# A scan layer's gate: projected before the scan and kept in DRAM, or projected behind the scan

## The chip, the cores and the metric

The kernel runs on one core of one Trainium2 chip. The metric is the device time of one launch in microseconds; of several executions the median is taken.

## What is computed

Four layers run one after the other on x of shape (8, 64, 64, 64). The change lies in the first, a selective-scan block. Cut to what matters, for each of 8 images with L = 4096 positions, 64 channels, an inner width of 128 and 16 states:

```python
xz = einsum('bhwc,dc->bhwd', ln(x), in_proj_w) + in_proj_b
xi, z = split(xz, 2, axis=-1)              # z: the gate
xc = silu(dwconv3(xi))
...                                        # four directions k of a scan over L:
h = h * exp(dt_t * A) + dt_t * B_t * u_t   # 128 channels x 16 states
y = sum over k of (C_t . h) + D * u
y = ln(y) * silu(z)                        # normalised over the 128 channels
xh = x + einsum('bhwd,cd->bhwc', y, outproj_w) + outproj_b
```

The layers that follow (a gate with attention, a modifier that is trained for some steps, another attention) take xh and are not touched.

## The kernel before

The scan layer (`scan_layer`, L242) handles the images one by one. An image's scan has 16 steps `s` (the loop at L928): four directions k, each with four chunks of 1024 positions. A step has 16 turns `n`, one for each state (the loop at L958). A turn holds, on its engines:

- ScalarE: `decay` (L733), the exponential for two turns ahead; `save_state` (L769).
- PE and ScalarE: `spread` for the next turn, which fills the PSUM tile z: for most states by matmuls (L751), for the states in `BY_POOL` (0, 3, 6, 8) by a copy of ScalarE (L748) from a product that GpSimd made (L741).
- VectorE: `unit`, a product z * dus in PSUM (L778, not for `BY_POOL`) and the scan (L782) into one of three h buffers.
- GpSimd: the product of h with the broadcast C row (L787); once a step two products for the next step's inputs (L659, L678).
- PE: `sum_up`, which adds that product of three turns before into y's PSUM tile (L848).
- SP: `load`, the broadcast loads of the B and C rows (L729), 512 KB each.

All other work is cut into items, pairs `(make, use)`, that a queue (`Background`, L166) hands out. In each turn `bg.before` calls one item's `make` (mostly a matmul into one of two PSUM banks, `bank`, L331); after the turn's scan `bg.after` first issues what was put off by `bg.later`, and then calls the `use` of the item of the turn before. In turns 6, 7 and 8 no item with a `make` is begun. Convolution parts stand in groups of their own, which alternate with the queue. The order of instructions is thus written out by hand; a tile scheduler adds only the semaphores.

The items that matter here:

- `before(b)` (L489) prepares an image while the image ahead of it is scanned: it loads x into the tile xn (one buffer), normalises it there (`norm_x`, L369), projects it for the convolution (`project_in`, L505), and for the gate: `gate` (L520) has a matmul from xn with the second half of `win` (L524), a Silu of ScalarE from PSUM into the SBUF tile z (L529), and a DMA that puts z into the DRAM tile zd (L530). The eight gates of an image stand in the queue behind its projections; for image 0 they are put in at step 4.
- `after(b)` (L566) finishes an image while the next one is scanned: from step 0 of the next image, turn 4, on. Its items come from `norm_y` (L426): variances of eight blocks of 512 positions (L438, put into the row tile vrow by ScalarE, L344, and into DRAM, L345), the chain over DRAM that makes the inverse root, then for each block `apply` (VectorE y * rps, L460; ScalarE Identity with the norm's scale and bias, L461), `multiply` (GpSimd z * y, L580), and `project_out` (two matmuls, L586 and L587, Identity L593, store L594). `load` (L571) fetches the block of x for the residual and the block of z (L575).
- The last image's blocks are finished two at a time in its own last three steps and behind the last scan; there a turn hands out two items.

An Exp, a Silu, a Ln and a Sqrt of ScalarE need different tables. Where one follows another, an ACT_TABLE_LOAD stands ahead of it.

Of the kernel before, what the change touches and what calls it, by code (L numbers as in the profile page):

```python
# [241 lines left out]
def scan_layer(cm, x_in, w, xh):  # L242

    tc, nc = cm.tc, cm.nc
    with ExitStack() as ctx:
# [177 lines left out]
                    out.append(none)  # L423
            return out

        def norm_y(y, blocks, load, multiply, project_out):  # L426

            put, chain, sm = inverse_root(len(blocks))
            j0, nb, sq = blocks[0], len(blocks), {}

            def square(j):
                sq[j] = work.tile([128, BK], F32, name="sq", tag="sq")
                nc.scalar.activation(sq[j], y[:, bass.ts(j, BK)], AF.Square)

            def variance(j):
                def make():
                    ps = bank("vps1")
                    nc.tensor.matmul(  # L438
                        ps[:1], lno_avg[:, NBK - 1 : NBK], sq.pop(j), start=True, stop=True
                    )  # L440
                    return ps

                def use(ps):
                    put(ps, 1, j - j0)
                    if j + 2 in blocks:
                        square(j + 2)

                return make, use

            def apply(j):  # L450
                def make():
                    ps = bank("rps")

                    row = cm.ident[:nb, j - j0 : j - j0 + 1].to_broadcast([nb, DI])
                    nc.tensor.matmul(ps, row, sm["r"], start=True, stop=True)
                    return ps

                def use(ps):
                    v = y[:, bass.ts(j, BK)]
                    nc.vector.tensor_tensor(v, v, ps, ALU.mult)  # L460
                    nc.scalar.activation(v, v, AF.Identity, bias=on_b, scale=on_g)  # L461
                    if j - 1 in blocks:
                        multiply(j - 1)

                return make, use

            out = [(None, lambda _: [square(j) for j in blocks[:2]]), none]
            for j in blocks:
                out.append(variance(j))
                if j in blocks[1:6:2] or nb == 2:  # L470
                    at = j if nb == 2 else j0 + (j - j0) // 2
                    out.append((None, lambda _, at=at: load(at)))
            out += chain
            out += [apply(j) for j in blocks[:2]]
            end = (None, lambda _: multiply(blocks[-1]))
            if nb == 2:
                out += [end, none]
            for j in blocks:
                if j + 2 in blocks:
                    out.append(apply(j + 2))  # L480
                    if j + 2 == blocks[-1]:
                        out.append(end)
                out += [project_out(j), none]
            return out


# [1 line left out]

        def before(b):  # L489

            xn = io.tile([2 * C, NBK // 2, BK], F32, name="xn", tag="xn", bufs=1)

            def block(j):
                e = j % 2
                return slice(e * C, (e + 1) * C), xn[e * C : (e + 1) * C, j // 2, :]
            u = io.tile([DI, L], F32, name="u", tag="u")
            zd = dr.tile([DI, L], F32, name="zd", tag="zd")
            rows = BK // S

            xs = x_in[b].rearrange("c h w -> c (h w)")  # L500
# [4 lines left out]
            def project_in(j):  # L505
                def make():
                    ps = bank("xps")
                    half, x = block(j)
                    nc.tensor.matmul(ps, win[half, 0, :], x, start=True, stop=True)
                    return ps  # L510

                def use(ps):
                    nc.scalar.activation(
                        pad[:, 1 + j * rows : 1 + (j + 1) * rows, 1 : S + 1],
                        ps.rearrange("p (r c) -> p r c", c=S), AF.Identity, bias=inb[:, 0:1],
                    )

                return make, use

            def gate(j):  # L520
                def make():
                    ps = bank("zps")
                    half, x = block(j)
                    nc.tensor.matmul(ps, win[half, 1, :], x, start=True, stop=True)  # L524
                    return ps

                def use(ps):
                    z = work.tile([DI, BK], F32, name="z", tag="z", bufs=3)
                    nc.scalar.activation(z, ps, AF.Silu, bias=inb[:, 1:2])  # L529
                    bg.later(lambda: nc.sync.dma_start(zd[:, bass.ts(j, BK)], z))  # L530

                return make, use

# [27 lines left out]
            items = [[(None, load(j)) for j in range(NBK)]]  # L561
            for pairs in FIRST if b == 0 else (range(NBK // 2),):
                items.append(norm_x(b, xn, pairs, project_in))
            return u, zd, items, [gate(j) for j in range(NBK)], [convolve(j) for j in range(NBK)]

        def after(b, y, zd, blocks=range(NBK)):  # L566

            xf = x_in[b].rearrange("c h w -> c (h w)")
            gated = {}
# [1 line left out]
            def load(j):  # L571
                xr = work.tile([C, BK], F32, name="xr", tag="xr", bufs=3)
                nc.sync.dma_start(xr, xf[:, bass.ts(j, BK)])
                z = work.tile([DI, BK], F32, name="z", tag="z", bufs=3)
                nc.sync.dma_start(z, zd[:, bass.ts(j, BK)])  # L575
                gated[j] = (xr, z)

            def multiply(j):
                z = gated[j][1]
                nc.gpsimd.tensor_tensor(z, z, y[:, bass.ts(j, BK)], ALU.mult)  # L580

            def project_out(j):
                def make():
                    po = bank("ops")
                    xr, z = gated[j]
                    nc.tensor.matmul(po[:C], cm.ident[:C, :C], xr, start=True, stop=False)  # L586
                    nc.tensor.matmul(po[:C], wout, z, start=False, stop=True)  # L587
                    return po

                def use(po):  # L590
# [6 lines left out]

                return make, use

            return norm_y(y, blocks, load, multiply, project_out)  # L600

        def ordered(t, k, c):

# [290 lines left out]
        later = {}  # L894

        def start(b):
            u, zd, items, gates, convs = before(b)
            images[b] = {"u": u, "zd": zd}
            bg.add(items[0] + items[1])
            if b == 0:  # L900
                bg.add(convs[0] + convs[1])
                for s in range(1, NCH):
                    later[s] = sum(items[s + 1 : s + 2], []) + convs[2 * s] + convs[2 * s + 1]
                later[NCH] = gates
            else:
                bg.done[b] = 0
                bg.add([(None, lambda _: bg.groups.extend(deque(conv) for conv in convs))])
                bg.add(gates)


        with tc.manual_schedule():
# [15 lines left out]
            for b in range(NB):  # L927
                for s in range(4 * NCH):  # L928
# [29 lines left out]
                    for n in range(N):  # L958
# [29 lines left out]

                        if s == 0 and n == LAG + 2 and b > 0:
                            last = images.pop(b - 1)  # L990
                            bg.add(after(b - 1, last["row"], last["zd"]))
                            bg.add([(None, lambda _, b=b - 1: bg.flushed.add(b))])
                        if late and n == LAG + 2:
                            c = 4 * NCH - s
                            bg.add(after(b, images[b]["row"], images[b]["zd"], range(2 * c, 2 * c + 2)))
                        if s == (1 if b else NCH) and n == 0 and b + 1 < NB:
                            bg.add(later.pop(NCH, []))
                            start(b + 1)
                    if nxt:
                        if not nxt["first"]:  # L1000
# [4 lines left out]
                sum_up()  # L1005
            empty()
            last = images[NB - 1]
            bg.add(after(NB - 1, last["row"], last["zd"], range(2)))
            bg.drain()


# [1146 lines left out]
```

## Time and profile before

| what | value |
|---|---|
| median of 3 runs | 12329.48 us (12318.48 to 12333.17) |
| profiled execution, its own time | 12328.75 us |
| span of the profiled execution | 12326.7 us, mean granted PE clock 0.952 |
| scan layer within the span | first scan at 94.4 us, last scan begins at 7016.3 us |
| image 2, first scan to next image's first | 856.3 us |
| DMA in all | 1562.16 MB, 38.5% of 16 engines' span |

The profile is one execution as the hardware profiler recorded it. The page's groups give for each line of the kernel the engine, the operation, its operands with their shapes, the count, and then behind the first bar the busy time in all and the mean time of one in ns, and behind the second bar how long the engine had stood idle just before these instructions and who ended that. A table of windows gives the busy time of each engine in a stretch of the span. A timeline lists an engine's instructions in order (start, duration, and in brackets the idle time ahead of it with its releaser; neighbours of one kind are merged).

### The profile page before, as it was taken

The page shows a single profiled execution, that of the slowest core. Times are in us where ns is not written, and L with a number is a line of the kernel's source. Part 1 is how long each engine was busy: PE and PEld are TensorE (multiplying, and loading weights), DVE is VectorE, ACT ScalarE, POOL GpSimd, SP SyncE. Part 2 cuts the span into 40 slices and gives each one's busy share as a digit, 9 for nine tenths or more (in the row PEclk, how much of TensorE's full clock was granted, in tenths as well). Part 3 has the DMA queues.
Part 4 walks back from the last instruction along what each step waited for, and adds up shares of the span by engine and source line. Part 5 has one row for each costly group of instructions (what it writes and reads, how often), then busy time and mean ns, then how long its engine had stood idle before and what let it go on. Part 6 is the DMA issues. An engine that isn't in the chain of part 4 may idle for free. (4 is left out here: it accounts for less than half of the span.)

```text
span 12326.7 us, 120038 instructions
## 1 busy us (share of the span) xinstructions
PE 11203.1 (91%) x38827; PEld 4075.9 (33%) x38827; DVE 10359.2 (84%) x7334; ACT 7820.8 (63%) x10409; POOL 7399.3 (60%) x3510
## 2 busy tenths in 40 slices
PE   7899999999999999999998899999987779999999
PEld 2233332332332332333322233232335463333333
DVE  5999999999999999999999776868677686676767
ACT  4776776776766766767766554646547574555554
POOL 5999999999999999999999700000006480000000
PEclk8999999999999999999999899999998789999999
DMA  3666666666666666666666400000011100000000
GB/s 115 207 213 218 209 209 217 219 203 216 218 210 213 211 210 217 213 215 213 199 213 211 164 24 26 5 25 7 17 41 41 41 21 24 19 4 19 5 11 6
DMA packets 541331, 1562.16 MB, mean 127 GB/s; under 512 B 127360, under 2 KB 144400, under 8 KB 538128
## 3 DMA queue, kind: packets, MB, share of 16 engines
q1 hardware_dynamic: 540688, 1554.36, 38.5%
q8 instruction: 309, 5.06, 0.2%
q14 instruction: 334, 2.74, 0.1%
HBM read 1456.41 MB, written 88.87 MB: 125 GB/s over the span
## 5 line engine op out<-in xcount | busy, mean ns | idle before, releaser
L787 POOL TENSOR_TENSOR ct<-ct,h 128x1024 f32<-128x1024 f32 x2048 | 4794.6, 2364 | 248.2 <-DVE h L782 113.3
L782 DVE TENSOR_TENSOR_SCAN h<-a,state,z 128x1024 f32<-128x1024 f32 x1536 | 3573.1, 2342 | 118.2 <-ACT z L748 67.1
L1159 DVE TENSOR_TENSOR sum<-sum,ex 128x1024 f32<-128x1024 f32 x1920 | 2347.5, 1223 | 618.1 <-ACT ex L1152 484.4
L1152 ACT ACTIVATE ex<-sc 128x1024 f32<-128x1024 f32 x2048 | 1968.1, 1024 | 1359.6 <-PE sc L1147 1359.6
L848 PE MATMUL yps<-ct,ident 128*128 128x512 f32 x5632 | 2809.0, 630 | 2.5 <-POOL ct L787 2.4
L733 ACT ACTIVATE a<-dt,amat 128x1024 f32<-128x1024 f32 x2048 | 2345.4, 1147 | 725.9 <-DVE h L782 712.5
L778 DVE TENSOR_TENSOR z<-z,e 128x1024 f32<-128x1024 f32 x1536 | 1863.3, 1213 | 221.1 <-PE z L751 143.2
L1166 PE MATMUL av<-ex,v 128*64 128x512 f32 x8192 | 1950.0, 604 | 0.0
L1147 PE MATMUL sc<-q,k 16*128 16x512 f32 (+1 forms) x8192 | 1562.2, 623 | 4.2 <-ACT q L1140 3.1
L848 PEld LDWEIGHTS yps<-ct,ident 128*128 128x128 f32 x5632 | 1006.4, 194 | 1384.2 <-issue 1220.6
L751 PE MATMUL z<-bs,pick 48*128 48x512 bf16 x3072 | 948.0, 389 | 536.5 <-DVE h L782 485.5
L848 PE MATMUL yps<-ct,lno_cen 128*128 128x512 f32 x2560 | 1276.3, 630 | 0.0
L782 DVE TENSOR_TENSOR_SCAN h<-a,z 128x1024 f32<-128x1024 f32 x512 | 1162.7, 2282 | 81.4 <-ACT z L748 57.2
L741 POOL TENSOR_TENSOR bt<-bt,e 128x1024 f32<-128x1024 f32 x512 | 1210.1, 2364 | 5.3 <-DMA bt<-bc 5.3
L1473 POOL TENSOR_TENSOR gt<-gt,pad 128x1024 f32<-128x1024 f32 x16 | 34.9, 2179 | 1570.2 <-ACT gt L1472 1570.2
L1166 PEld LDWEIGHTS av<-ex,v 128*64 128x64 f32 x8192 | 512.2, 136 | 1332.8 <-issue 1278.9
L1147 PEld LDWEIGHTS sc<-q,k 16*128 16x128 f32 (+1 forms) x8192 | 528.4, 184 | 1016.2 <-issue 977.3
L748 ACT COPY z<-bt 128x1024 f32<-128x1024 f32 x512 | 519.8, 1015 | 537.5 <-POOL bt L741 334.8
L751 PEld LDWEIGHTS <-pick 48*128 48x128 bf16 x3072 | 177.6, 95 | 1754.9 <-DVE h L782 1003.0
L848 PEld LDWEIGHTS yps<-ct,lno_cen 128*128 128x128 f32 x2560 | 458.1, 193 | 618.3 <-issue 564.2
L544 PE MATMUL vps<-pad,convd 128*128 128x512 f32 x1152 | 550.9, 602 | 12.9 <-ACT e L648 12.9
L1846 DVE RECIPROCAL r<-e 128x512 f32<-128x512 f32 x128 | 420.7, 3323 | 0.0
(416 smaller groups left out, 10449.5 us busy)
## 6 DMA issues: line engine op xcount, KB each, us to landing
ct<-bc SPq DMA_DIRECT2D x2048, 512.0 KB
bt<-bc SPq DMA_DIRECT2D x512, 512.0 KB
x<-x SPq DMA_DIRECT2D x12, 2048.0 KB
bc<-e SPq DMA_DIRECT2D x128, 128.0 KB
zd<-z SPq DMA_DIRECT2D x64, 256.0 KB
z<-zd SPq DMA_DIRECT2D x64, 256.0 KB
x<-x SPq DMA_DIRECT2D x32, 512.0 KB
part<-x SPq DMA_DIRECT2D x128, 128.0 KB
```

What stands on the lines that cost most here:

```text
L544: nc.tensor.matmul(held[0].rearrange("p (r c) -> p r c", c=S), convd[:, t, :], pad[:, j * rows + dy : (j + 1) * rows + dy, dx : dx + S], s ...
L733: ctl["exp", n] = nc.scalar.activation(ctl["a", n], ctl["dt"], AF.Exp, scale=amat[:, ctl["k"], n : n + 1])
L741: nc.gpsimd.tensor_tensor(bt, bt, ctl["dus"], ALU.mult)
L751: nc.tensor.matmul(z[:, bass.ts(i, BK)], pick[:, n : n + 1].to_broadcast([3 * N, DI]), ctl["bs"][:, bass.ts(i, BK)], start=True, stop=True,)
L778: first = nc.vector.tensor_tensor(z, z, ctl["dus"], ALU.mult)
L782: nc.vector.tensor_tensor_scan(h[:, flip], a[:, flip], z[:, flip], 0.0 if state is None else state[:, n : n + 1], ALU.mult, ALU.add,)
L787: freed[at] = nc.gpsimd.tensor_tensor(ct, ct, h, ALU.mult)
L848: nc.tensor.matmul(ctl["ps"][:, bass.ts(i, BK)], ctl["mat"], ct[:, bass.ts(i, BK)], start=False, stop=(n == N - 1 and not ctl["turns"]),)
L1147: nc.tensor.matmul(sc[:, e, :], k[r : r + d, bass.ts(j, 128)], qs[i][r : r + d, :], start=True, stop=True,)
L1152: nc.scalar.activation(ex, sc, AF.Exp)
L1159: nc.vector.tensor_tensor(sums[i], sums[i], ex, ALU.add)
L1166: nc.tensor.matmul(avs[i][r, :], v[:, j, r], ex[:, e, :], start=(j == 0), stop=(j == TQ - 1))
```

## The change

- The gate is no longer made in `before` and no longer put into DRAM: zd, its 64 stores and 64 loads are gone, and the SBUF tile z with them.
- xn gets two buffers, so that an image's normalised input is still there when its scan has ended.
- `after` has a new `gate(j)`: its `make` has the matmul from xn with `win` into a PSUM bank, and puts off a Silu in place in that bank to the end of the turn; its `use`, one turn later, is a product on VectorE of the bank and y's block, written into y.
- GpSimd's `multiply` is gone; `project_out` reads y instead of z.
- In `norm_y` the gates stand one in a row of three: apply, gate, project. The separate items for `load` are gone; the first three blocks of x are fetched in the `use` of the first three variances.

The core of the diff (the rest are the signatures and the call sites that hand on `block` in place of `zd`):

```diff
@@ norm_y
                     if j + 2 in blocks:
                         square(j + 2)
+                    if j - j0 < 3:
+                        load(j)
...
                     nc.scalar.activation(v, v, AF.Identity, bias=on_b, scale=on_g)
-                    if j - 1 in blocks:
-                        multiply(j - 1)
...
             for j in blocks:
                 out.append(variance(j))
-                if j in blocks[1:6:2] or nb == 2:
-                    at = j if nb == 2 else j0 + (j - j0) // 2
-                    out.append((None, lambda _, at=at: load(at)))
             out += chain
-            out += [apply(j) for j in blocks[:2]]
-            end = (None, lambda _: multiply(blocks[-1]))
-            if nb == 2:
-                out += [end, none]
+            out += [apply(j) for j in blocks[:2]] + [gate(j0)]
             for j in blocks:
                 if j + 2 in blocks:
                     out.append(apply(j + 2))
-                    if j + 2 == blocks[-1]:
-                        out.append(end)
-                out += [project_out(j), none]
+                out += [gate(j + 1) if j + 1 in blocks else none, project_out(j)]
@@ before
-            xn = io.tile([2 * C, NBK // 2, BK], F32, name="xn", tag="xn", bufs=1)
+            xn = io.tile([2 * C, NBK // 2, BK], F32, name="xn", tag="xn")
...
-            zd = dr.tile([DI, L], F32, name="zd", tag="zd")
...
-            def gate(j):
-                def make():
-                    ps = bank("zps")
-                    half, x = block(j)
-                    nc.tensor.matmul(ps, win[half, 1, :], x, start=True, stop=True)
-                    return ps
-
-                def use(ps):
-                    z = work.tile([DI, BK], F32, name="z", tag="z", bufs=3)
-                    nc.scalar.activation(z, ps, AF.Silu, bias=inb[:, 1:2])
-                    bg.later(lambda: nc.sync.dma_start(zd[:, bass.ts(j, BK)], z))
@@ after
-                z = work.tile([DI, BK], F32, name="z", tag="z", bufs=3)
-                nc.sync.dma_start(z, zd[:, bass.ts(j, BK)])
-                gated[j] = (xr, z)
-
-            def multiply(j):
-                z = gated[j][1]
-                nc.gpsimd.tensor_tensor(z, z, y[:, bass.ts(j, BK)], ALU.mult)
+                gated[j] = xr
+
+            def gate(j):
+                def make():
+                    ps = bank("zps")
+                    half, x = block(j)
+                    nc.tensor.matmul(ps, win[half, 1, :], x, start=True, stop=True)
+                    bg.later(lambda: nc.scalar.activation(ps, ps, AF.Silu, bias=inb[:, 1:2]))
+                    return ps
+
+                def use(ps):
+                    v = y[:, bass.ts(j, BK)]
+                    nc.vector.tensor_tensor(v, ps, v, ALU.mult)
...
-                    xr, z = gated[j]
-                    nc.tensor.matmul(po[:C], cm.ident[:C, :C], xr, start=True, stop=False)
-                    nc.tensor.matmul(po[:C], wout, z, start=False, stop=True)
+                    v = y[:, bass.ts(j, BK)]
+                    nc.tensor.matmul(po[:C], cm.ident[:C, :C], gated[j], start=True, stop=False)
+                    nc.tensor.matmul(po[:C], wout, v, start=False, stop=True)
```

In the changed kernel the Silu is at L558, VectorE's gate product at L563, the product y * rps still at L462 and the scan at L767.

## The prediction, made before the changed kernel had run

> **What bounds the kernel now.** I read the page first (busy shares and largest groups), then a table of engine busy time by image, then the idle times in VectorE's own timeline, each with its releaser, image by image, and last what ScalarE was doing at those moments. Everything that the change touches runs in the scan layer, the first 7050 us. I count images 0 to 7, in each 16 steps of 1024 positions, in each step 16 turns n (one scan, L782, is one turn).
>
> The page: the costliest group on each engine.
> ```profile
> PE 11203.1 (91%) x38827; PEld 4075.9 (33%) x38827; DVE 10359.2 (84%) x7334; ACT 7820.8 (63%) x10409; POOL 7399.3 (60%) x3510
> ...
> L787 POOL TENSOR_TENSOR ct<-ct,h 128x1024 f32<-128x1024 f32 x2048 | 4794.6, 2364 | 248.2 <-DVE h L782 113.3
> L782 DVE TENSOR_TENSOR_SCAN h<-a,state,z 128x1024 f32<-128x1024 f32 x1536 | 3573.1, 2342 | 118.2 <-ACT z L748 67.1
> ...
> L778 DVE TENSOR_TENSOR z<-z,e 128x1024 f32<-128x1024 f32 x1536 | 1863.3, 1213 | 221.1 <-PE z L751 143.2
> ```
> Busy time in one image (image 2, from its first scan to the next image's first).
> ```profile
> core 0: us, PE busy (x) PEld busy (x) DVE busy (x) ACT busy (x) POOL busy (x), PEclk, DMA share, GB/s
> ...
> 1868.60:2724.90 856.30, 799.37 (x1824) 271.89 (x1824) 818.62 (x463) 615.34 (x881) 835.78 (x377) 0.97 0.65 213
> ```
> GpSimd is busy 835.8 of 856.3 us and VectorE 818.6: two engines nearly full, neither with room for much. That alone would say "take work off GpSimd and gain". The timeline says otherwise. A turn lasts 3.5 us (scan 2.35 + product 1.21) or 2.3 us (products that GpSimd makes), so VectorE runs back to back and paces the turns; GpSimd follows with a lag, and only where the lag uses up the three h buffers does VectorE stand still. Adding up VectorE's listed idle times in images 1 to 5 gives 27.6 us an image: 10.8 released by PE's z (L751), 7.2 by ScalarE's z (L748), only 6.6 by GpSimd's ct (L787). So what counts is a list of stalls. Those that the change can touch, in VectorE's timeline:
> ```profile
> 404.93 2.29 DVE L782 TENSOR_TENSOR_SCAN h<-a,z 128x1024 f32<-128x1024 f32 x1 [6.28 <-ACT z L748]
> ```
> ```profile
> 2113.26 1.23 DVE L778 TENSOR_TENSOR z<-z,e 128x1024 f32<-128x1024 f32 x1 [1.25 <-POOL ct L787]
> ```
> ```profile
> 2211.53 2.35 DVE L782 TENSOR_TENSOR_SCAN h<-a,state,z 128x1024 f32<-128x1024 f32 x1 [2.75 <-ACT z L748]
> ```
> ```profile
> 2472.84 1.23 DVE L778 TENSOR_TENSOR z<-z,e 128x1024 f32<-128x1024 f32 x1 [2.49 <-PE z L751]
> ```
> The bracket is the idle time and who ended it. They lie in step 4 of image 0 (eight gates in consecutive turns), and in steps 4, 6 and 11 of image 2. The third is not what it seems. ScalarE's z copy was late because a copy ahead of it had waited for a DMA (its own timeline):
> ```profile
> 2209.95 0.57 ACT L344 COPY vrow<-vps 2x512 f32<-2x512 f32 x1 [5.18 <-DMA vard<-vrow]
> 2210.43 1.00 ACT L748 COPY z<-bt 128x1024 f32<-128x1024 f32 x1
> ```
> vrow has one buffer, and two variances in successive turns make the second wait until the first is in DRAM.
>
> **What the Trainium skill says.** "SBUF — State Buffer", section "Who interferes with whom": a VectorE instruction with at most one SBUF input does not contend with GpSimd, one with two SBUF inputs does. The new product reads PSUM and y, so GpSimd's L787 should keep its 2364 ns; the trace has no contrary case, since every large VectorE product here reads one operand from PSUM. "ScalarE: Activation LUTs", section "What ACT_TABLE_LOAD costs": about 1283 ns for each load plus some 1380 ns of drain. The trace agrees on 1283 (row below) but shows no such drain: at 402.86 an Exp starts 1.29 us after its load began, at 401.57. I use 1.28. The same page (section "Step-by-step: what each stage is for") holds that ScalarE writes faster into PSUM; I take no gain for the Silu from it.
>
> **The change, part by part.** Prices, from the groups of the scan layer:
> ```profile
> L529 ACT ACT_TABLE_LOAD x64 | 82.1, 1283 | 1.1
> L580 POOL TENSOR_TENSOR z<-z,y 128x512 f32<-128x512 f32 x64 | 81.5, 1273 | 23.3 <-ACT y L461 23.3
> ...
> L529 ACT ACTIVATE z<-zps,inb 128x512 f32<-128x512 f32 x64 | 44.0, 688 | 4.4 <-PE zps L524 3.6
> L460 DVE TENSOR_TENSOR y<-y,rps 128x512 f32<-128x512 f32 x64 | 42.2, 663 | 6.9 <-PE rps L455 6.9
> ```
> (a) VectorE gets 64 products y = zps*y. L460 has the same shape and the same places (one operand PSUM, result SBUF): 64 x 0.663 = +42.4 us. In steps 3 and 4 the turns with an L460 now last 4.1 instead of 3.5 us, so an added product lengthens its turn in full: nothing hides it. 5.3 us an image.
>
> (b) GpSimd loses 64 x 1.273 = 81.5 us. What of it comes back is only the idle time that GpSimd's lag causes on VectorE near those products: in images 1 to 5, steps 3, 4, 5: 1.15 + 2.5 + 0.3 = 4.0 us an image, and 1.0 us at turn 4 of step 5, where PE's z is late behind a sum that waited for the late ct. Images 6 and 7: 5.1 and 4.5. Sum 5 x 5.0 + 9.6 = -35 us. VectorE's longer turns give GpSimd further time, so I take all of it; the least would be half.
>
> (c) The Silu and its matmul move from steps 9 to 11 of the image before into steps 2 to 4, behind the scan. Their number stays (64 Silus, 64 loads), and so does that of the loads that bring Exp back. Each costs ScalarE 1.28 + 0.69 + 1.28 = 3.25 us. In the order of instructions the convolutions now come one in a step from 9 to 15. What goes: VectorE idles 2.1, 0.75 and 3.5 us in steps 9, 10, 11 (6.3), against 1.6 in a step with one convolution alone whose parts begin in turns 3 to 5 (13 to 15), and less where they begin at turn 9, which is likely in 9 and 10 because the projections hold the early turns. I expect 0.7 + 0.7 + 1.6 = 2.9 left: -3.4 x 5 = -17. Image 0: its burst of eight gates goes, 6.3 + about 1 = -7. Image 6, where convolutions come in pairs, idles 27.9 us in steps 9 to 13; with a third fewer loads there I put 20: -8. Sum -32.
>
> (d) What the moved Silus cost where they land. They stand at turns 13, 15 of step 2; 4, 10, 13 of step 3; 2, 5, 10 of step 4. In turns 9 to 15 a gate has stalled nothing: six a image stand there now, at 3.5 us a turn. Three now fall into turns 2 to 5, which also hold z copies and step sizes; but ScalarE idles 2.7 and 4.0 us at turn 4 of steps 3 and 4, waiting for GpSimd's bt. Bounds: 0, and 3.25 us each; I take 1 us an image, +7. The product on VectorE is a new wait, for the Silu and for y's Identity; behind it stand the next turn's z product and scan, and behind those all engines. The Silu is issued a turn earlier (2 us of 3.5), so the wait should be nothing outside (f). PSUM: the bank is held until VectorE's product, at the end of the next turn; PE now waits for VectorE in turns where it waited for no one, 0.66 us of the about 1 us that it has free; I count nothing.
>
> (e) Variances. Without the load items between them they stand in turns 5, 6, 10, 11, 12 of step 1 where they stood in 5, 6, 10, 11, 13, 14: three waits either way, nothing. But the rest of the queue comes three slots earlier, and in step 6 the last two variances of the next image now stand in turns 0 and 3 instead of 3 and 4: the wait of 5.18 us goes, and with it the stall: 2.35 us an image in images 1 to 5, 1.9 in image 6: -13.7. Should it turn up elsewhere, 0.
>
> (f) The last image's own gates stand in turn 13 and 14 of steps 13, 14, 15, two at once. The second Silu waits for the state copy of scan 13, then load and Silu follow the Exp of its turn: ready about 8.9 us after scan 13, while VectorE reaches its product at 5.6: 3.3 us idle, less 0.8 that goes with GpSimd's products: 2.5 x 3 = +7.5. In the tail the chain has Silus between Identities: 4.3 + 0.66 against 3.4 us: +1.5. Sum +9.
>
> (g) DMA: 64 writes and 64 loads of 256 KB fewer (33 of 1562 MB), and 128 issues fewer on SP, some 0.4 us each, which waits for ct buffers anyway (PE's L848): nothing. xn has two buffers; the load for the image after next waits for a gate matmul issued before it: nothing.
>
> Sum: 42.4 - 35 - 32 + 7 - 13.7 + 9 = -22 us. The profiled execution took 12328.75 us (span 12326.7 and 2 us around it), within 1 us of the median 12329.48, so I forecast 12307 us.
>
> **Rivals.** First: GpSimd was the pace, being fuller than VectorE, and its whole 81.5 us comes back, VectorE's products fitting into its idle time: 12248. For it: GpSimd runs without a gap through steps 3 and 4 (55.1 of 55.1 and 54.5 of 54.5 us in image 1). Against it: the 6.6 us of waits above, and turns of exactly VectorE's length. Second, on the other side: the table loads in turns 2 to 5 are not covered, because the cover was ScalarE's wait for the lagging GpSimd. Three gates an image at the full 3.25 us, in seven images, are 68 instead of 7 us: 12368. It decides from 47 more us, that is (7 + 22 + 25) / 21 = 2.6 us for each such gate, to show as slower; with half of (b) lost as well, from 1.7 us. In step 11 the gate at turn 5 goes with about 1.9 us more idle time than in steps 13 to 15, which speaks for it. Third: the change leaves all as it was, because what (b), (c) and (e) give is just what (a) takes: 12330.
>
> **How the numbers follow.** About 0.2%, 25 us, is what a measurement here can tell from no change. Forecast, with its own range 12285 to 12322: 0.55, a little under half of it below 12305. GpSimd as the pace: 0.2. Exposed loads: 0.17. No change: 0.08. So faster 0.25 + 0.2 = 0.45, same 0.3 + 0.08 = 0.38, slower 0.17. Range 12255 to 12348: towards the first rival nearly in full, and half-way to the second, since three exposed loads at their whole price in every image are the bound.
>
> **What would show it.** L563 on VectorE near 0.66 us, 64 times; no "POOL ct" release of VectorE in steps 3 to 5; GpSimd about 825 us an image, VectorE about 823; step 6 without the vrow wait and its stall; step 4 of image 0 near 52 us instead of 58.3. I am wrong if steps 2 to 4 together, now about 162.5 us, come out over 167 (rival two) or under 156 (rival one), or if steps 9 to 11 keep their 6.3 us of idle time.

## The result, and the profile after

The changed kernel takes 12360.7 us (median of 19 runs, 12342.4 to 12382.6) against 12331.4 us for the kernel before in the same session: ratio 1.0026, 95% interval 1.0020 to 1.0032. By the ratio it is slower by 32 us. The forecast was 12307 us with a range of 12255 to 12348: both the sign and the range were wrong.

First the pace of the engines. The page of the changed kernel, the lines that answer to those shown of before:

```profile
PE 11222.1 (91%) x38827; PEld 4078.7 (33%) x38827; DVE 10400.5 (84%) x7398; ACT 7820.4 (63%) x10409; POOL 7326.8 (59%) x3446
...
L772 POOL TENSOR_TENSOR ct<-ct,h 128x1024 f32<-128x1024 f32 x2048 | 4797.3, 2364 | 346.8 <-DVE h L767 135.6
L767 DVE TENSOR_TENSOR_SCAN h<-a,state,z 128x1024 f32<-128x1024 f32 x1536 | 3571.6, 2342 | 96.5 <-ACT z L733 50.3
```

and image 2, from its first scan to the next image's first:

```profile
core 0: us, PE busy (x) PEld busy (x) DVE busy (x) ACT busy (x) POOL busy (x), PEclk, DMA share, GB/s
1864.51:2725.46 860.95, 801.21 (x1824) 271.62 (x1824) 823.47 (x472) 616.26 (x882) 827.47 (x369) 0.97 0.63 207
```

The work moved as foreseen: VectorE went from 818.6 to 823.5 us in this image (forecast 823), GpSimd from 835.8 to 827.5 (forecast 825), and GpSimd's idle time before L772 rose from 248 to 347 us, so it is further from setting the pace. Still the image takes 861.0 us where it took 856.3. What grew is idle time. The moved operations, in the groups of the scan layer:

```profile
L558 ACT ACT_TABLE_LOAD x62 | 79.5, 1283 | 26.9 <-PE zps L557 25.9
...
L563 DVE TENSOR_TENSOR y<-zps,y 128x512 f32<-128x512 f32 x64 | 43.0, 672 | 18.0 <-ACT zps L558 17.9
L462 DVE TENSOR_TENSOR y<-y,rps 128x512 f32<-128x512 f32 x64 | 42.6, 667 | 14.0 <-PE rps L457 13.9
L558 ACT ACTIVATE zps<-zps,inb 128x512 f32<-128x512 f32 x64 | 42.4, 662 | 48.9 <-PE zps L557 48.0
...
L344 ACT COPY vrow<-vps 1x512 f32<-1x512 f32 x64 | 36.7, 573 | 72.6 <-DMA vard<-vrow 55.9 <-PE vps L438 12.9 <-PE yps L833 3.8
...
L344 ACT COPY vrow<-vps 2x512 f32<-2x512 f32 x32 | 18.3, 571 | 7.6 <-DMA vard<-vrow 6.6 <-PE vps L390 1.0
```

The new product costs about what L460 cost (0.672 against 0.663 us, 64 times). In the kernel before, the Silu and its load had 5.5 us of idle time ahead of them; here they have 75.8 us, nearly all of it waiting for PE's gate matmul. The vrow copies of two rows, which had waited 32.4 us for the DMA, wait 6.6; those of one row still wait 55.9 (76.1 before). The same copies in the kernel before:

```profile
L344 ACT COPY vrow<-vps 1x512 f32<-1x512 f32 x64 | 36.7, 573 | 91.4 <-DMA vard<-vrow 76.1 <-PE vps L438 15.2
...
L344 ACT COPY vrow<-vps 2x512 f32<-2x512 f32 x32 | 18.3, 572 | 33.3 <-DMA vard<-vrow 32.4 <-PE vps L390 0.9
```

Where this meets VectorE: image 2, step 3, turn 5, VectorE's timeline, then ScalarE's, then PE's.

```profile
2046.80 2.35 DVE L767 TENSOR_TENSOR_SCAN h<-a,state,z 128x1024 f32<-128x1024 f32 x1
2049.06 0.67 DVE L563 TENSOR_TENSOR y<-zps,y 128x512 f32<-128x512 f32 x1
2050.58 2.35 DVE L767 TENSOR_TENSOR_SCAN h<-a,state,z 128x1024 f32<-128x1024 f32 x1 [0.85 <-ACT z L733]
```

```profile
2042.81 0.19 ACT L754 COPY state<-h 128x1 f32<-128x1 f32 x1
2046.88 1.28 ACT L558 ACT_TABLE_LOAD   x1 [3.87 <-PE zps L557]
2048.17 0.66 ACT L558 ACTIVATE zps<-zps,inb 128x512 f32<-128x512 f32 x1
2048.76 0.80 ACT L463 ACTIVATE y<-y,on_b,on_g 128x512 f32<-128x512 f32 x1
2049.47 1.01 ACT L733 COPY z<-bt 128x1024 f32<-128x1024 f32 x1
2050.49 1.28 ACT L718 ACT_TABLE_LOAD   x1
```

```profile
2043.39 1.98 PE L833 MATMUL yps<-ct,ident 128*128 128x512 f32 x4
2045.68 1.12 PE L557 MATMUL zps<-xn,win 64*128 64x512 f32 x2 [0.30 <-DVE y L462]
```

The Silu is issued in the turn of its own matmul (L557), which stands on PE behind that turn's sum of ct (L833). ScalarE takes its instructions in the order written: it stands for 3.87 us, and only then load, Silu and y's Identity go by and z is copied (L733), which the next scan needs. The scan at 2050.58 is late by 0.85 us. The forecast had said that ScalarE idles here anyway (2.7 us, for GpSimd's bt) and would have room. It idles here indeed, but *ahead of* the Silu.

For the account the lengths of the steps were taken from the starts of the scans. To see how well they repeat, each kernel was profiled a second time (below); the table has the mean of both profiles, images 1 to 5.

| steps | before, us | after, us | difference | forecast |
|---|---|---|---|---|
| 0, 1 | 108.4 | 107.8 | -0.6 | 0 |
| 2 to 4 | 162.8 | 169.7 | +6.9 | +2.7 |
| 5 to 7 | 160.4 | 156.8 | -3.6 | -3.7 |
| 8 | 50.3 | 52.5 | +2.3 | 0 |
| 9 to 11 | 160.0 | 158.7 | -1.3 | -3.4 |
| 12 | 51.3 | 51.0 | -0.3 | 0 |
| 13 to 15 | 159.6 | 161.4 | +1.8 | 0 |
| sum | 852.7 | 857.8 | +5.1 | -4.4 |

The forecast's column is its steps (a) to (e) put where they act: in 2 to 4, 5.3 - 1.15 - 2.5 + 1. Over five images this is +25 instead of -22 us: 48 of the 63 us by which the profiles differ from the forecast's sum. Image 0 gave 3.9 (forecast 7), image 6 2.9 (forecast 8.7); image 7 and what follows the last scan took 15.2 + 7.1 more (forecast 16 together). The spans' means differ by 41 us, the medians of the timed runs by 29 to 32.

### The profile page after: what moved, and what is told of

Same layout as the page of the kernel before. It is cut to its first block, busy times and chain, and to the rows that moved or that the text cites. A ratio compares the mean times of both kernels' runs of the same rounds, so it can differ in the third digit from the quotient of the medians.

```text
span 12365.2 us, 119784 instructions
## 1 busy us (share of the span) xinstructions
PE 11222.1 (91%) x38827; PEld 4078.7 (33%) x38827; DVE 10400.5 (84%) x7398; ACT 7820.4 (63%) x10409; POOL 7326.8 (59%) x3446
## 5 line engine op out<-in xcount | busy, mean ns | idle before, releaser
L772 POOL TENSOR_TENSOR ct<-ct,h 128x1024 f32<-128x1024 f32 x2048 | 4797.3, 2364 | 346.8 <-DVE h L767 135.6
L767 DVE TENSOR_TENSOR_SCAN h<-a,state,z 128x1024 f32<-128x1024 f32 x1536 | 3571.6, 2342 | 96.5 <-ACT z L733 50.3
L833 PE MATMUL yps<-ct,ident 128*128 128x512 f32 x5632 | 2803.9, 629 | 0.4 <-POOL ct L772 0.4
L833 PEld LDWEIGHTS yps<-ct,ident 128*128 128x128 f32 x5632 | 1003.8, 193 | 1375.6 <-issue 1221.3
L833 PE MATMUL yps<-ct,lno_cen 128*128 128x512 f32 x2560 | 1286.9, 635 | 0.0
L767 DVE TENSOR_TENSOR_SCAN h<-a,z 128x1024 f32<-128x1024 f32 x512 | 1162.9, 2282 | 80.1 <-ACT z L733 59.8
L726 POOL TENSOR_TENSOR bt<-bt,e 128x1024 f32<-128x1024 f32 x512 | 1210.1, 2364 | 5.4 <-DMA bt<-bc 5.4
L733 ACT COPY z<-bt 128x1024 f32<-128x1024 f32 x512 | 519.9, 1015 | 559.0 <-POOL bt L726 265.8
L833 PEld LDWEIGHTS yps<-ct,lno_cen 128*128 128x128 f32 x2560 | 462.4, 195 | 622.5 <-issue 561.7
```

The source lines that it names most:

```text
L726: nc.gpsimd.tensor_tensor(bt, bt, ctl["dus"], ALU.mult)
L767: nc.vector.tensor_tensor_scan(h[:, flip], a[:, flip], z[:, flip], 0.0 if state is None else state[:, n : n + 1], ALU.mult, ALU.add,)
L772: freed[at] = nc.gpsimd.tensor_tensor(ct, ct, h, ALU.mult)
L833: nc.tensor.matmul(ctl["ps"][:, bass.ts(i, BK)], ctl["mat"], ct[:, bass.ts(i, BK)], start=False, stop=(n == N - 1 and not ctl["turns"]),)
```

## The experiments

Theory after the result: *the Silu costs where it lands* (rival two of the prediction), through ScalarE. Rivals: the product on VectorE costs more than its 0.66 us, by the waits that it adds; or neither, and the shifted queue puts other items into worse turns. All ratios are against the kernel before, with 95% intervals.

**Without the product, without the Silu.**

The first leaves y ungated:

```diff
                 def use(ps):
-                    v = y[:, bass.ts(j, BK)]
-                    nc.vector.tensor_tensor(v, ps, v, ALU.mult)
+                    pass
```

The second multiplies y with the raw projection:

```diff
-                    bg.later(lambda: nc.scalar.activation(ps, ps, AF.Silu, bias=inb[:, 1:2]))
```

> The changed kernel without VectorE's gate product: matmul and Silu stay, but y is left ungated, so this leaves the gate out of the result. Theory W (ScalarE stands still because it is given the Silu in the same turn as the gate's matmul, and is late for what follows) and theory V (the products on VectorE are the cost, all else is small) both put the product itself at 64 x 0.67 = 43 us on the path; the changed kernel stands at 1.0026 of before. If the product is wholly exposed this gives 0.9991 of before (about -43 us from the changed kernel). If VectorE's products fall into waits that are there anyway, it stays near 1.0026 and theory V falls. Under W the step 3 and 4 waits of ScalarE for the gate's matmul stay.

> The changed kernel without the Silu and its table loads: VectorE multiplies y with the raw projection, so the Silu is left out of the result. Theory W: ScalarE no longer waits for PE inside a turn, the 4 us of idle time of VectorE in steps 3 and 4 of each image go, and 3 x 3 us in the last image: about -35 us from the changed kernel, ratio 0.9998. Theory V: only the waits of the last image go, about -8 us, ratio 1.002. Theory S (the loss sits in steps 8, 9 and 13 to 15 because the queue's items stand in other turns): as V, and those steps keep their excess.

Measured: 0.9980 [0.9972, 0.9988] and 0.9983 [0.9976, 0.9991]. Each gives back more than the whole loss. The product is worth 57 us, of which 43 are its own busy time. The Silu with its loads is worth 53 +- 12 us, where the forecast had some 16 for it ((d) and most of (f)). Without the Silu, steps 2 to 4 take 163.7 us in images 1 to 5: 0.9 more than before, which is the product's 5.3 less 4.4 for GpSimd. So (a) and (b) hold, and 6.0 us an image go with the Silu.

Turn by turn (start of one scan to start of the next, medians over the images of the two profiles of the changed kernel and of the one without Silu) the difference in steps 2 to 4 is 6.8 us, and 5.6 of it lie in turns 5 and 6 of step 3 and turns 4 to 7 of step 4. There ScalarE runs three of the image's eight Silus, in turn 5 of step 3 and turns 3 and 6 of step 4. These are the three that the forecast had named; all other turns of the three steps together have 1.2 us.

**The Silu into SBUF, a turn later, and the product by GpSimd or by VectorE.**

```diff
-                    bg.later(lambda: nc.scalar.activation(ps, ps, AF.Silu, bias=inb[:, 1:2]))
...
                 def use(ps):
+                    z = work.tile([DI, BK], F32, name="z", tag="z", bufs=2)
+                    nc.scalar.activation(z, ps, AF.Silu, bias=inb[:, 1:2])
                     v = y[:, bass.ts(j, BK)]
-                    nc.vector.tensor_tensor(v, ps, v, ALU.mult)
+                    bg.later(lambda: nc.gpsimd.tensor_tensor(v, z, v, ALU.mult))
```

The second of the two has `nc.vector` in the place of `nc.gpsimd`. In both, the last image's first project_out comes one item later.

> The gate is projected behind the scan, but the Silu is issued one turn after its matmul and goes into an SBUF tile, and GpSimd multiplies one turn later, as in the kernel before. Against the changed kernel: the VectorE products go (-43 us) and GpSimd's lag in steps 3 to 5 comes back (+25 to +35 us). Theory W: the waits of ScalarE for PE go too, -28 us: ratio 0.9992 to 1.0000. Theory V: the waits were small: 1.0015 to 1.002. Theory S: as V.

> As the run with GpSimd's product, but VectorE multiplies, now with both inputs in SBUF. Theory W: -28 us from the changed kernel, ratio 1.0003, if the product stays at 0.67 us and GpSimd's products at 2.364 us. Theory V: 1.0026. If two SBUF inputs make VectorE and GpSimd wait for each other, the product's mean time exceeds 0.7 us or GpSimd's L772 group exceeds 2364 ns, and the ratio rises over 1.0026.

Measured: 1.0001 [0.9992, 1.0009] and 1.0043 [1.0029, 1.0057]. With GpSimd's product and the later Silu nothing is left of the loss, and nothing is gained. The second shows why the product has to read PSUM:

```profile
L565 DVE TENSOR_TENSOR y<-z,y 128x512 f32<-128x512 f32 x64 | 95.5, 1493 | 4.1 <-ACT z L563 4.1
```

The same product with both operands in SBUF takes 1493 instead of 672 ns in the mean; single ones take from 665 to 5514 ns, and the two with no GpSimd instruction beside them, in the tail, 0.68 and 0.69 us. This is the contrary case that was missing for what the prediction took from the Trainium skill ("SBUF — State Buffer", "Who interferes with whom"): with two SBUF operands VectorE contends with GpSimd, with one it doesn't. The trace agrees (1493 against 672 ns); the price is on VectorE, while GpSimd's large product goes from 2364 to 2372 ns.

**The Silu in PSUM as in the change, issued at the start of the next turn.**

The instruction goes into a list that `Background.before` empties first of all:

```diff
+        early, self.early = self.early, []
+        for do in early:
+            do()
...
-                    bg.later(lambda: nc.scalar.activation(ps, ps, AF.Silu, bias=inb[:, 1:2]))
+                    bg.early.append(lambda: nc.scalar.activation(ps, ps, AF.Silu, bias=inb[:, 1:2]))
```

> The changed kernel with one move: the Silu is issued at the start of the next turn, behind that turn's z copy, instead of at the end of the turn in which PE makes the projection; the product stays at the end of the next turn. Table loads and products stay as many. Theory W (ScalarE stands still for PE inside a turn, and z's copy is late behind it): 2 to 4 us an image in steps 2 to 4, -15 to -25 us from the changed kernel, ratio 1.0007 to 1.0014. Theory L (the load, the Silu and the second load are simply too much for ScalarE in these turns, 3.25 us each wherever they stand): no gain, 1.0026, as VectorE's product then waits for the Silu.

Measured: 1.0006 [0.9998, 1.0015]: 25 of the 53 us come back, with nothing changed but when ScalarE gets the instruction. Its groups:

```profile
L562 ACT ACT_TABLE_LOAD x62 | 79.5, 1283 | 3.4 <-PE zps L561 2.3
...
L567 DVE TENSOR_TENSOR y<-zps,y 128x512 f32<-128x512 f32 x64 | 43.2, 676 | 24.2 <-ACT zps L562 24.2
...
L562 ACT ACTIVATE zps<-zps,inb 128x512 f32<-128x512 f32 x64 | 42.3, 662 | 4.0 <-PE zps L561 3.2
```

ScalarE's 75.8 us of idle time ahead of load and Silu fall to 7.4. The product on VectorE now waits longer for the Silu itself (24.2 against 18.0 us), and the kernel is faster all the same; steps 2 to 4 take 166.8 us. So what hurt was less the product's wait than what stood behind ScalarE's. The wait is not all of it: against the kernel without Silu, 3.1 us an image in steps 2 to 4 stay (166.8 against 163.7), for the loads and the product's wait together.

**Identity in the place of Silu: the loads by themselves.** The activation stays where it is, with its wait; only the two table loads around each go.

```diff
-                    bg.later(lambda: nc.scalar.activation(ps, ps, AF.Silu, bias=inb[:, 1:2]))
+                    bg.later(lambda: nc.scalar.activation(ps, ps, AF.Identity, bias=inb[:, 1:2]))
```

The second run has the same edit in the kernel before, at L529.

> The changed kernel with Identity in the place of the gate's Silu: the output is not the reference's, the in-order wait of ScalarE for PE's gate matmul stays, the table loads go. Leaving the whole activation out gave 0.9983; issuing it one turn later gave 1.0006; the changed kernel stands at 1.0026. If the wait itself is what costs 25 us or more: 1.0012 or more, 12347 us. If the wait is harmful only because the load and the load back to Exp come behind it: 0.999 or less, 12321 us.

> The kernel before with Identity in the place of the gate's Silu: the output is not the reference's, the activation stays with its size and its place, and the table loads that the Silu and the next Exp need are gone. What do the gates' loads in steps 9 to 11, in image 0 and image 6 cost the kernel before? By the forecast's step (c) they are what the change was to save there, 32 us: 0.9974, 12300 us. Rival: ScalarE has room for them except in image 0's burst of eight, 7 us, so the change had little to gain there: 0.9992 or more, 12323 us.

Measured: 0.9999 [0.9990, 1.0008] and 0.9977 [0.9970, 0.9985]. The first lies between the two cases that were set out, nearer to the second. The loads cost the changed kernel 33 +- 13 us, and they had cost the kernel before 28 +- 9 us. This is the core of the case: step (c) was right that the gates' loads cost about 32 us where they stood, and step (d) wrong that the moved Silus cost 7 where they went. The two costs can't be told apart. That the wait alone is nearly harmless is seen in the same turn of the changed kernel with Identity (ScalarE, then VectorE):

```profile
2037.04 0.66 ACT L558 ACTIVATE zps<-zps,inb 128x512 f32<-128x512 f32 x1 [3.46 <-PE zps L557]
2037.63 0.80 ACT L463 ACTIVATE y<-y,on_b,on_g 128x512 f32<-128x512 f32 x1
2038.33 1.01 ACT L733 COPY z<-bt 128x1024 f32<-128x1024 f32 x1
```

```profile
2037.38 2.35 DVE L767 TENSOR_TENSOR_SCAN h<-a,state,z 128x1024 f32<-128x1024 f32 x1
2039.64 0.67 DVE L563 TENSOR_TENSOR y<-zps,y 128x512 f32<-128x512 f32 x1
2040.23 2.34 DVE L767 TENSOR_TENSOR_SCAN h<-a,state,z 128x1024 f32<-128x1024 f32 x1
```

ScalarE waits 3.46 us, as with Silu (3.87), but z is copied 1.3 us after the wait ends and not 2.6, and the scan at 2040.23 follows the product at once. It is wait and load in a row that overrun the turn. Either one taken away gives 25 to 33 us. Over steps 2 to 4 the medians of the turns with Identity come to those without any activation (0.2 us less). Their mean does not, 165.7 against 163.7 us, because of one image of 174.3; the other four take 162.5 to 164.6.

**A second buffer for vrow.** The prediction saw step 6's stall and counted step 1 as "three waits either way, nothing". vrow had shared its one buffer with the row rstd; the edit gives it two of its own.

```diff
-                t = work.tile([NBK, BK], F32, name="vrow", tag="rstd", bufs=1)
+                t = work.tile([NBK, BK], F32, name="vrow", tag="vrow", bufs=2)
```

> The kernel before with two buffers for vrow, nothing else. The prediction put 2.35 us an image in step 6 and this reading puts 3.8 us in step 1 on the wait for vrow's DMA: 6.1 us x 6 images, -37 us, ratio 0.997, and ScalarE's 76 us of waits for that DMA go. If these stalls have another cause, or another wait takes their place (the z copy then waits for GpSimd's bt): under half of that, 0.9985 or more.

> The changed kernel with a second buffer for vrow and nothing else. In the kernel before, the same edit was worth 22 us (4.2 us an image in step 1, 2.3 in step 6), in the changed kernel with the later Silu 39 us. If the change had taken the stall of step 6 and left that of step 1, as the order of the variances says, the edit is worth the 4.2 us an image of step 1 alone and some of the last image: 0.9998, 12330 us. If the wait for vrow is larger in the changed kernel because its variances stand closer together (no load items between them): 39 us as with the later Silu, 0.9994, 12322 us. If the two edits of that kernel help one another: under 15 us, 1.0015 or more.

> As the run before it, and vrow gets two buffers of its own, so that a variance no longer waits until the one before is in DRAM. In the changed kernel the wait before the third z copy of step 1 costs VectorE 3.5 us an image. If that reading of the chain is right: another -20 to -25 us, ratio 0.9987 to 0.9997. If the late z copy has another cause: as a_silu_next.

Measured: in the kernel before 0.9982 [0.9975, 0.9988], in the changed kernel 0.9998 [0.9989, 1.0006], in the changed kernel with the later Silu 0.9974 [0.9965, 0.9984], 12298.4 us. The wait is gone (kernel before with two buffers):

```profile
L344 ACT COPY vrow<-vps 1x512 f32<-1x512 f32 x64 | 36.6, 572 | 17.2 <-PE vps L438 17.0
...
L344 ACT COPY vrow<-vps 2x512 f32<-2x512 f32 x32 | 18.3, 571 | 1.8 <-PE vps L390 1.8
```

In the kernel before it took 4.1 us an image from step 1 and 2.1 from step 6 (steps 2 and 7 give 1.8 back); for step 6 the prediction had 2.35. In the changed kernel step 1 gains 3.2 and step 6 nothing, since its stall is gone already. So (e) was right in place; step 1's wait stayed, and in image 2 it stalls a scan by 4.30 us, more than the 3.45 of before (kernel before, then changed kernel):

```profile
1948.17 2.35 DVE L782 TENSOR_TENSOR_SCAN h<-a,state,z 128x1024 f32<-128x1024 f32 x1 [3.45 <-ACT z L748]
```

```profile
1945.72 2.35 DVE L767 TENSOR_TENSOR_SCAN h<-a,state,z 128x1024 f32<-128x1024 f32 x1 [4.30 <-ACT z L733]
```

By the timed runs the edit is worth 34 and 39 us in the two changed kernels, and 22 in the kernel before; by the intervals that difference is not settled. The last of the three beats both kernels: by its ratio it is 32 us below the kernel before, and 64 below the changed one. Against the kernel before with the same second buffer (0.9982), moving the gate with the later Silu is then worth about 10 us, which the intervals can't tell from nothing.

**Empty items, so that the queue keeps its old turns.** Three empty items between the variances, where the loads had stood, and eight behind the projections of the next image, where the gates had stood (in the last image, one behind each variance).

```diff
                 out.append(variance(j))
+                if j in blocks[1:6:2] or nb == 2:
+                    out.append(none)
...
+                bg.add([none] * NBK)
```

> The changed kernel with empty items in the queue: three where norm_y had its load items, eight where the gates stood, so that the next image's normalisation and its convolutions stand in the turns of the kernel before. Theory S (the excess of steps 8 and 13 to 15, some 5 us an image in the changed kernel's profile, comes from items in other turns): steps 8 and 13 to 15 return to 50.4 and 53.1 us in the mean of images 1 to 5, step 6 returns to 53.7 us: near 1.002. If the excess is chance in PE's clock, these steps stay as spread as they are, and the ratio rises to 1.003 with step 6's stall.

> The changed kernel with both edits: the Silu is issued at the start of the next turn instead of at the end of the matmul's own turn, and the 11 empty items stand where the loads and the gates stood, so that the rest of the queue has its old turns again. Each edit alone took about 24 us off the changed kernel (1.0006 and 1.0007 of before, against 1.0026). Theory that these are two causes (ScalarE waits in order for PE's gate matmul; the convolutions and the other items of the queue fall into other turns): the gains add up, 0.9987 +- 0.001, 12312 us. Rival: they are one cause, the empty items helped only because they moved the Silus to other turns: no further gain, 1.0006, 12335 us.

> All three edits in the changed kernel: later Silu, second vrow buffer, 11 empty items. With two buffers the variances no longer wait, so the three empty items between them should be worth nothing and only the eight later ones count. If the turns of the convolutions and of the other items matter by themselves: below the 0.9974 of the kernel without the empty items, 0.996 or less, 12280 us. If the empty items only moved Silus and variances, both of which are mended here: 0.9974, 12299 us.

Measured: 1.0007 [0.9999, 1.0016], then 1.0023 [1.0014, 1.0033] and 1.0003 [0.9994, 1.0011]. The first looked like a second cause next to the Silu's. The other two refute that reading, and the rivals set out with it: with the Silu mended the same items *cost* 21 and 36 us. The steps show two effects at once. Step 8, 52.5 us in the changed kernel, is back at 50.2, 50.2 and 51.0 us in the three kernels (50.3 in the kernel before). That the shifted queue alone makes it long is not shown: with the later Silu, or with GpSimd's product, it takes 50.8 us without any empty item. But the first three items push the gates back, so that steps 3 and 4 have four each, where steps 2 to 4 had two, three and three, and in step 3 VectorE now waits for PE (image 2, changed kernel with the empty items alone, VectorE's timeline):

```profile
2043.46 1.23 DVE L765 TENSOR_TENSOR z<-z,e 128x1024 f32<-128x1024 f32 x1 [1.26 <-PE z L738]
...
2050.27 0.69 DVE L462 TENSOR_TENSOR y<-y,rps 128x512 f32<-128x512 f32 x1 [0.96 <-PE rps L457]
```

Steps 2 to 4 take 168.4 instead of 166.8 us with the later Silu, and 170.8 instead of 166.1 with the second buffer as well. Steps 13 to 15 stay long (161.0 to 162.4). Why the items gained 23 us where the Silu was not mended is not settled: at the same time they moved the Silus that ScalarE had run in turns 3, 5 and 6 to turns 0 and 4, and the two can't be told apart here.

**Both kernels once more, for their profiles.**

> The kernel before once more, for its profile alone: how far do the lengths of the 16 steps, as a mean over images 1 to 5, differ between two profiles of the same kernel? If they repeat within 0.3 us, the 2.6 us that the changed kernel has more in step 8 and in steps 13 to 15 are its own. If they wander by a microsecond or more, that part of the account says nothing.

> The changed kernel once more, for its profile alone, with the same question: steps 2 to 4 at 169.3, step 8 at 53.0 and steps 13 to 15 at 161.9 us again, each within 0.3 us, if these are properties of the kernel; step 8 near 51 and steps 13 to 15 near 160 if they are chances of one execution.

Spans 12319.9 us (12326.7 in the first profile) and 12363.7 (12365.2). Steps 2 to 4: 162.5 and 163.0 before, 169.3 and 170.0 after: repeatable. Step 8: 50.4 and 50.1 against 53.0 and 52.0. Steps 9 to 11 wander by 1.5 us before and 1.2 after, 13 to 15 by 0.7 and 1.1; single images by up to 12 us. So single numbers of the second half carry about a microsecond that does not repeat.

Most of this goes with the clock that PE was granted, which the trace records. In images 1 to 6 it falls to half for 3.4 us or a multiple of that, and meanwhile a 128x512 matmul that sums up ct (L848, kernel before) takes 1061 instead of 592 ns (medians). In images 1 to 5 the steps sort themselves by their time at half clock:

- Steps 13 to 15 take 159.4 to 159.9 us in images with 6.8 us at half clock, 161.8 to 162.3 with 13.7, and 165.3 in the one with 20.5. Both kernels do so alike. The changed kernel has more of it (11.6 us an image in the mean, before 7.5), and its +1.8 goes with that.
- Step 8 has none of it in the kernel before (50.1 to 51.3 us). In the changed kernel seven of the ten images have 3.4 to 7.3 us of it and take 51.8 to 55.5 us; the other three take 50.5, 50.5 and 52.5.
- In steps 9 to 11, with 3.4 us of it, one image of the kernel before takes 158.6 us and four of the changed kernel 156.8 to 157.1.
- Steps 2 to 4 have 8.9 us of it before, 13.0 in the changed kernel and 6.8 without the Silu, so some of the 6.0 us put down to the Silu goes with the clock. Most does not: with the same 10.2 us of it, three images take 162.4 to 162.9 us before and three 167.2 to 169.3 in the changed kernel; the one without the Silu (10.3 us) takes 164.0.

A whole image has 47.8 us at half clock in the changed kernel and 41.6 before. Whether the order of PE's work brings this about, its waits, or chance, no run here shows.

Over all ten profiles with the change's queue unpadded (with and without Silu, product or buffer), step 8 averages 52.1 us, steps 9 to 11 158.2, steps 13 to 15 160.8; over those of the kernel before and its variants 50.3, 160.1 (without the one with Identity, whose loads are missing there) and 159.7. Together that is +1.0 us an image where -3.4 was forecast.

## Why the prediction was wrong, step by step

- **(a) Product, +42.4:** right in size, 43.0 us busy at 672 ns. Leaving it out gives 57 us. With it go its waits for ScalarE (17.9 us) and PE's waits for it, which the prediction had counted as nothing (11.5 us ahead of the project_out matmul L571); what each of them costs was not tested.
- **(b) GpSimd's relief, -35:** right. Without the Silu, steps 2 to 4 show 4.4 us an image against 3.65 foreseen there, and of VectorE's idle time in them GpSimd's ct ends 0.2 and 0.1 us an image (the two profiles) where it ended 3.9 and 3.6. Rival one, 12248, is refuted: GpSimd lost 73 us of work and the kernel is slower.
- **(d) Moved Silus, +7: the step that failed.** The prediction said: "Three now fall into turns 2 to 5 ... but ScalarE idles 2.7 and 4.0 us at turn 4 of steps 3 and 4", and took 1 us an image between 0 and 9.75 (three at 3.25). Measured in steps 2 to 4: 6.0 us an image, nearly all of it at these three. The idle time was counted as room without asking where in it the Silu would stand. It was put behind a matmul of its own turn, so the room went by in waiting, and load, Silu and the load back came after it, when z was due. The sentence "The Silu is issued a turn earlier (2 us of 3.5), so the wait should be nothing outside (f)" looked at VectorE's wait for ScalarE, and not at ScalarE's for PE.
- **(c) Loads out of steps 9 to 11, -32:** right in two places, too large in the third. Image 0's burst went as foreseen: its step 4 takes 51.2 and 51.1 us (the two profiles) where it took 58.3 and 60.3, forecast 52. The 3.9 us of the whole image hide this, since its other steps differ by 7 us between the two profiles of the changed kernel. Image 6 gained 8.6 us in steps 9 to 13 (forecast 8) and lost most of it in steps 2 to 4. In images 1 to 5 steps 9 to 11 gave 1.3 to 1.9 us and not 3.4. The forecast had laid 3.4 of their 6.3 us of idle time to the gates, without asking who ended it. Of that time ScalarE ended only 2.0 us, PE's z 4.0. ScalarE's part fell to 0.4 in the changed kernel, just as in the kernel before with Identity; PE's was 4.0 and 2.1 before and is 4.1 and 3.0 now. All told (c) gave some 23 to 26 of its 32 us.
- **Steps 8 and 13 to 15, no term:** they became 2.3 and 1.8 us longer an image. The prediction saw that the queue comes earlier and put a price only on vrow. The excess goes with PE's time at half clock; what brings that about is open.
- **(e) vrow:** step 6 as foreseen in kind (its stall is gone; step 6 itself is 1.1 us shorter; with steps 5 and 7 the sum is -3.6 against -3.65), step 1 rightly unchanged. But the larger part of that wait was in step 1 and stood there for the taking.
- **(f) Last image, +9:** with what else falls there, 22 us against 16. The kind is right, the second of two gates waits for its Silu:

```profile
6984.94 0.67 DVE L563 TENSOR_TENSOR y<-zps,y 128x512 f32<-128x512 f32 x1
6988.82 0.69 DVE L563 TENSOR_TENSOR y<-zps,y 128x512 f32<-128x512 f32 x1 [3.21 <-ACT zps L558]
```

The forecast had 3.3 us for this wait.
- **Rival two, 12368**, was nearest in time and right in its mechanism, exposed loads behind turns 2 to 5. Its price was too high: it put 68 us on them, and measured in steps 2 to 4 are 6.0 us in each of images 1 to 5, 7.0 in image 6 and 1.9 in image 7, 39 in all. That it came out at nearly the measured time is luck: (c) fell short as well, and steps 8 and 13 to 15 grew. The prediction's own mark, steps 2 to 4 over 167 us, decided rightly for it.

In the timed runs the Silu's 53 us against 16 is 37 of the 54 us between forecast and measurement; the rest, about 17, is the changed kernel without Silu (21 us below before, where the forecast's own terms give 38), and lies in (c) and in steps 8 and 13 to 15.

## What to carry to other kernels

Before you count an engine's idle time as room for a moved instruction, ask what that instruction itself waits for: on an engine that works in order the wait eats the room, and the work behind it has only what is left. Moving a cost that belongs to the instruction, such as a table load, from one nearly full stretch to another moves the cost; only taking it away, or giving the instruction data that are already there (here: one turn later), saved some of it. When you price what goes away, count only the idle time that its own engine ends. Before you explain a microsecond that a step has gained or lost, look at the granted clock in it. A queue with written-out order has no neutral shift: here eleven empty items were worth -23 or +36 us, depending on what else stood in those turns.

## What was not expected of the hardware

- A 128x512 product on VectorE with both operands in SBUF took 1493 ns in the mean beside a busy GpSimd, and 672 ns with one in PSUM.
- The Silu that writes into PSUM took 662 ns, the one into SBUF 688 (in the kernel before) and 687. The Trainium skill ("ScalarE: Activation LUTs", "Step-by-step: what each stage is for") says that ScalarE writes faster into PSUM; the trace agrees, with 26 ns of 688.
- Two profiles of one kernel, less than 0.1% apart in span, differ by up to 12 us in single images of about 860 us (image 3 of the kernel before: 847.7 us at a mean granted clock of 0.98, and 859.4 at 0.96). A claim on one image from one profile is worth little below that.
